# Who issues the weight loads of the late experts, when, and in which order, in a transformer block with routed experts

## The chip, the core and the metric

One Trainium2 chip, one core. The time is that of one execution on the device, in microseconds (us); lower is better. The engines are named as in the profile: PE (TensorE), DVE (VectorE), ACT (ScalarE), POOL (GpSimd) and SP (SyncE). DMA transfers are moved by 16 DMA engines that all queues share; q1 is the queue that SP issues into, q10 that of ACT, q0 that of POOL.

## The reference, cut to what matters

```python
x = x + attention(x) @ Wout.T                     # 16 sequences of 256 tokens, D = 256, 16 heads of 64
tok = x.reshape(-1, d)                            # 4096 tokens
gate = softmax(tok @ Wgate.T)                     # E = 8 experts
vals, idx = top_k(gate.T, bs // E)                # every expert takes its 512 best tokens
g = layernorm(tok[idx]) * mlp_g + mlp_b
y = gelu(einsum('ked,ehd->keh', g, fc1s) + b1s)   # 256 -> 1024
y = einsum('keh,edh->ked', y, fc2s) + b2s         # 1024 -> 256
tok = tok.at[idx].add(y * vals)
```

All numbers are float32. fc1 and fc2 of one expert are 1 MB each, b2 is spread over the partitions to 128 KB.

## The kernel before

The first 760 us are attention, ordered by a plan with a long table of places; at its end the routing finds each expert's tokens in two halves, so that there are 16 **jobs**: jobs 0 to 7 are the eight experts on their first 256 tokens, jobs 8 to 15 the same experts on the second 256. Job 0 is in the plan too; jobs 1 to 15 are a loop written out by hand (L1569 to L1622).

A job has 16 **slots**. In slots 0 to 7 `up` (L1273, tile `ph`) multiplies by fc1, 4 matmul passes each, and ACT follows with `gelu` (L1285, tile `hid`). In slots 8 to 15 `down` (L1293, tile `py`) multiplies by fc2, first for the job's tokens 0 to 127, then for the others; DVE finishes each half (L1304, `y`) and POOL adds it to `out` in DRAM with an indirect DMA (`scatter`, L1310). While job k computes, the tokens of job k+1 are brought:

- `list_matmul` (L1186, `pls`) and `take` (L1195) make the list of tokens. For the late jobs, k+1 from 9 to 15 (the flag `exchanged`), this is in slot 0; for the earlier ones in slot 5 (slot 7 once).
- `gather` (L1202, `xg`): two indirect DMAs by POOL, 128 tokens each.
- The tokens must be turned. Early jobs do it on PE in slot 14 (`transposes`, L1211, `px`). Late jobs do it by an **exchange** in slot 6: DVE turns blocks of 32 (`turn`, L1236, `xb`), SP writes them to DRAM (`away`, L1243, `xblocks`) and reads them back across the partitions in pieces of 512 bytes (`back`, L1250, `xT`). In slot 13 ACT scales `xT` (`affine`, L1258), in two halves; the next job's first `up` needs the first of them.

`load` (from L1138) brings a job's weights: fc2 into `w2`, which takes one of two buffers of the attention's tag `oT`; fc1 into `w1`, one of two buffers of tag `v`; then b2. It stands at the end of job k for job k+2 (`far`), when the buffers of job k have just come free, and all of it is issued by SP. SP works in order: a DMA that waits for its buffer holds all that stand behind it. The loads of jobs 0 and 1 are in the plan, that of job 2 ahead of the loop.

Of the kernel before, what the change touches and what calls it, by code (L numbers as in the profile page):

```python
# [9 lines left out]
F32 = mybir.dt.float32  # L10
# [8 lines left out]
P = 128  # L19
B, N, D = 16, 256, 256  # L20
# [9 lines left out]
FC = DD // P  # L30
# [16 lines left out]
class Plan:  # L47
# [7 lines left out]
    def step(self, place, engine, took, run, needs=(), makes=(), tiles=(), mode=0, lag=0.1):  # L55
        k = len(self.steps)
        self.steps.append((place, engine, took, run, needs, tiles, mode, lag))
        for m in makes:
            self.makers.setdefault(m, []).append(k)
# [7 lines left out]
def kernel(  # L67
# [18 lines left out]
    nc = tc.nc  # L86
# [338 lines left out]
    if True:  # L425
# [4 lines left out]
        moe = ctx.enter_context(tc.tile_pool(name="moe", bufs=2))  # L430
# [79 lines left out]
        class Through:  # L510


            def load(self):
                self.w = {}
                for c in range(DC):
                    self.w[c] = work.tile([P, H * HD], F32, tag="prT", bufs=4, name="wn")
                    nc.sync.dma_start(self.w[c], woutN[bass.ts(c, P), :])
# [614 lines left out]
        class Job:  # L1132
# [2 lines left out]
                self.oh = self.xT = None  # L1135
                self.exchanged = False

            def load(self):  # L1138


                e = self.e
                self.w2 = seq.tile([P, FC, D], F32, tag="oT", name="w2")
                nc.sync.dma_start(self.w2, fc2T[e].rearrange("(f p) d -> p f d", p=P))
                self.w1 = seq.tile([P, DC, DD], F32, tag="v", bufs=2, name="w1")
                rows = fc1Q if self.exchanged else fc1T
                nc.sync.dma_start(self.w1, rows[e].rearrange("(c p) f -> p c f", p=P))
                self.b2 = moe.tile([P, D], F32, tag="b2", bufs=2, name="b2")
                nc.sync.dma_start(self.b2, b2s[:, bass.ts(e, D)].to_broadcast([P, D]))

            def gives(self, engine=nc.vector):  # L1150

# [201 lines left out]
        for b in range(B):  # L1353
# [20 lines left out]
            else:  # L1374
                mr, xT_, wide, rows, hT = ("mr", b), ("xT", b), ("wide", b), ("rows", b), ("hT", b)
                f = base + FIRST[0]
# [36 lines left out]
            for d in range(HP // 2):  # L1413
                a = Quad(b, d)
                p = base + d * QUAD
# [25 lines left out]
            for t in range(TB):  # L1441
                a = Tail(b, t)
                p = base + TAIL[t]
# [60 lines left out]
        for n in range(2):  # L1504
            a = jobs[n]
            k = top + 10 + 20 * n
# [4 lines left out]
            for i in range(10):  # L1511
                name, took, by = {"D": ("DVE", 0.49, nc.vector), "P": ("POOL", 2.55, nc.gpsimd), "A": ("ACT", 2.1, nc.scalar)}[who[i]]
# [9 lines left out]
            for c in range(DC):  # L1522
                name, took, by = ("ACT", 0.55, nc.scalar) if c == 0 or n else ("DVE", 0.48, nc.vector)
# [4 lines left out]
        k = top + 30  # L1528
# [26 lines left out]
        def lay_out(job):  # L1555

            job.gives()
            for a in list(range(0, 18, 2)) + list(range(18, NT, 3)):
                yield
                job.onehot(a, a + (2 if a < 18 else 3))  # L1560
# [8 lines left out]
        for k in range(1, len(jobs)):  # L1569
            a = jobs[k]  # L1570
            new = jobs[k + 1] if k + 1 < len(jobs) else None
            far = jobs[k + 2] if k + 2 < len(jobs) else None
            late = k == last + 1
            list_at = LATE_AT if late else LIST_AT if new and new.exchanged else 5
            for s in range(SLOTS):
                for step in next(rest, ()):
                    step()
                if late and s == 0:
                    new.gives()
                if late and s < 6:  # L1580
                    new.onehot(6 * s, 6 * s + 6)
                if new and s == list_at:
                    for _ in () if late else parts:
                        pass
                    new.list_matmul(0, NT)
                    new.take()
                    new.gather()
                    if k == 1:
                        jobs[0].scatter(by_end[1])
                if s == 0:  # L1590
                    for step in held:
                        step()
                    held = []
                if new and new.exchanged:
                    for what in EXCHANGE.get(s, ()):
                        getattr(new, what)()
                elif new and s == TURN_AT:
                    new.transposes()
                    new.evict()
                if not late and s < list_at:  # L1600
                    next(parts, None)
                if far and k != last and s > list_at:
                    if s == list_at + 1:
                        parts = lay_out(far)
                    for _ in range(2 if far.exchanged and list_at else 1):
                        next(parts, None)
                if s < FC:
                    a.up(s)
                    a.gelu(s)
                    if s == FC - 1:  # L1610
                        a.weigh()
                else:
                    i, q = divmod(s - FC, 4)
                    a.down(i, 2 * q, 2 * q + 2)
                    if q == 3:
                        a.finish(i)
                        if far and far.exchanged and i == KL - 1:
                            held = [partial(a.scatter, i)]
                        else:
                            a.scatter(i)  # L1620
            if far:
                far.load()  # L1622
        assert next(rest, None) is None

# [57 lines left out]
```

## Time and profile before

| | |
|---|---|
| median of 3 runs | 1033.66 us (1032.98 to 1035.72) |
| profiled execution | 1033.8 us, of which the trace spans 1032.1 |
| PE busy | 998.3 us (97%) |
| DVE, POOL, ACT busy | 812.1, 657.4, 569.6 us |
| the loop of jobs (first `up` of job 0 to the last `down`) | 774 to 1022 us |
| jobs 9 to 15 and job 8 ahead of them | 900 to 1022 us |

The rest of the span, from 1022 us on, is the last scatters and the end of the program. The time of the profiled execution lies 0.14 us above the median, and 1.7 us of it lie outside the traced span.

### The profile page before, as it was taken

To read this page: it belongs to the slowest core of one execution; us is meant where nothing else is said; L and a number is where in the kernel's file an instruction comes from. 1 tells how busy PE (TensorE), PEld (TensorE's weight loads), DVE (VectorE), ACT (ScalarE), POOL (GpSimd) and SP (SyncE) were. 2 spreads that over 40 slices of the span, in tenths; PEclk is the share of its full clock that TensorE was granted. 3 is DMA by queue.
4 is the path that set the end of the run, shared out by engine and by line. 5 is a ranking of instruction groups with operands and counts; after the bars stand their busy time and mean duration, and the time that the engine had idled before them with its cause. 6 is when DMAs were issued, how large, how long until landed. Compare 5 with 4: busy or idle time off the path is not lost. (4 is left out here: it accounts for less than half of the span.)

```text
span 1032.1 us, 21313 instructions
## 1 busy us (share of the span) xinstructions
PE 998.3 (97%) x6803; PEld 606.7 (59%) x6803; DVE 812.1 (79%) x2271; ACT 569.6 (55%) x1596; POOL 657.4 (64%) x1003
## 2 busy tenths in 40 slices
PE   8999999999999999999999999998689999999996
PEld 6434455454554545455454545565468888888885
DVE  3789998899988889888898999887875888654630
ACT  2577766767667675766756766775214223233231
POOL 3699788788878787887878787765223333333332
PEclk9999999999999999999999999999889999999998
DMA  8456676676766767676776777677033557468662
GB/s 288 111 138 169 167 186 163 176 176 169 187 167 164 169 174 186 167 176 164 182 189 163 186 179 171 152 195 221 11 108 121 149 180 207 139 221 244 196 199 30
DMA packets 166144, 174.02 MB, mean 169 GB/s; under 512 B 18832, under 2 KB 154768, under 8 KB 166032
## 3 DMA queue, kind: packets, MB, share of 16 engines
q1 hardware_dynamic: 158512, 162.88, 58.8%
q0 software_dynamic: 6144, 8.39, 4.4%
q10 hardware_dynamic: 1376, 1.38, 0.4%
q8 instruction: 55, 0.90, 0.4%
q14 instruction: 57, 0.47, 0.1%
HBM read 59.57 MB, written 14.45 MB: 72 GB/s over the span
## 5 line engine op out<-in xcount | busy, mean ns | idle before, releaser
L441 PE MATMUL pm<-wq,hT 128*64 128x512 f32 x1536 | 352.7, 596 | 3.2 <-DVE qk L706 2.3
L787 ACT ACTIVATE pr<-sc,nmax 128x256 f32<-128x256 f32 x512 | 237.7, 479 | 119.7 <-DVE nmax L774 77.7
L798 POOL TENSOR_SCALAR pr<-pr,sums 128x256 f32<-128x256 f32 x512 | 237.5, 483 | 66.7 <-DVE sums L794 49.1
L112 POOL TENSOR_TENSOR ss<-ss,neghalf 128x8 f32<-128x8 f32 x128 | 210.8, 1647 | 10.7
L441 PEld LDWEIGHTS pm<-wq,hT 128*64 128x64 f32 x1536 | 106.5, 137 | 184.2 <-issue 146.3
L774 DVE TENSOR_REDUCE nmax<-sc 128x2 f32<-128x512 f32 x256 | 166.6, 670 | 11.3 <-PE sc L766 10.9
L808 DVE STREAM_TRANSPOSE pb<-pr 128x512 f32<-128x512 f32 x248 | 167.9, 692 | 6.5 <-POOL pr L798 5.8
L766 PE MATMUL sc<-kT,qT 64*128 64x256 f32 x1024 | 133.0, 392 | 0.6 <-ACT pr L787 0.6
L848 PE MATMUL po<-prT,v 128*64 128x256 f32 x1024 | 130.4, 384 | 0.1
L441 PE MATMUL pw<-wo,oT 128*64 128x264 f32 x1024 | 127.3, 391 | 0.5 <-DVE qk L706 0.5
L766 PEld LDWEIGHTS sc<-kT,qT 64*128 64x128 f32 x1024 | 93.8, 186 | 57.9 <-issue 24.8
L1310 POOL DMA_INDIRECT out<-y,idx x32 | 51.2, 1599 | 119.1 <-DVE oh L1178 55.8
L1273 PE MATMUL ph<-xT,w 128*128 128x256 f32 x512 | 118.8, 388 | 1.9 <-ACT xT L1258 1.9
L689 ACT ACTIVATE sq<-pm 128x512 f32<-128x512 f32 x128 | 77.2, 604 | 75.7 <-PE pm L441 74.9
L1293 PE MATMUL py<-w,hid 128*128 128x256 f32 x512 | 115.2, 380 | 0.4 <-ACT hid L1285 0.4
L848 PEld LDWEIGHTS po<-prT,v 128*64 128x64 f32 x1024 | 72.6, 137 | 68.8 <-issue 37.9
L693 DVE TENSOR_REDUCE ss<-sq 128x8 f32<-128x512 f32 x128 | 85.6, 670 | 32.8 <-ACT sq L689 32.0
L787 ACT ACTIVATION_READ_ACCUMULATOR pr<-sc,nmax 128x1 f32 x512 | 107.4, 210 | 0.0
L1273 PEld LDWEIGHTS ph<-xT,w 128*128 128x128 f32 x512 | 96.0, 192 | 16.1 <-ACT xT L1258 2.8
L1293 PEld LDWEIGHTS py<-w,hid 128*128 128x128 f32 x512 | 96.1, 190 | 13.6 <-ACT hid L1285 0.5
L706 DVE TENSOR_TENSOR qk<-pm,ss 128x512 f32<-128x512 f32 x128 | 86.9, 679 | 20.8 <-POOL ss L112 19.3
L1285 ACT ACTIVATE hid<-ph,vec 128x256 f32<-128x256 f32 x128 | 60.3, 474 | 74.2 <-PE ph L1273 65.1
(152 smaller groups left out, 1008.1 us busy)
## 6 DMA issues: line engine op xcount, KB each, us to landing
prT<-pb SPq DMA_DIRECT2D x496, 128.0 KB
qraw<-kb SPq DMA_DIRECT2D x128, 128.0 KB
kT<-kb SPq DMA_DIRECT2D x128, 128.0 KB
w<-in_fc2T SPq DMA_DIRECT2D x16, 1024.0 KB
w<-in_fc1T SPq DMA_DIRECT2D x9, 1024.0 KB
w<-in_fc1Q SPq DMA_DIRECT2D x7, 1024.0 KB
xT<-in_xT SPq DMA_DIRECT2D x16, 256.0 KB
out<-tok SPq DMA_DIRECT2D x32, 128.0 KB
```

What stands on the lines that cost most here:

```text
L112: nc.gpsimd.tensor_tensor(dst, src, neghalf[:, : src.shape[1]], ALU.pow)
L441: nc.tensor.matmul(out[cols], weights[:, cols], moving, start=start, stop=stop)
L693: nc.vector.tensor_reduce(self.ss[:, 0, :], self.sq.rearrange("p (q e d) -> p e q d", q=QB, e=8), AX.XY, ALU.add,)
L706: nc.vector.tensor_tensor(self.qk.rearrange("p (q e d) -> p q e d", q=QB, e=8), self.pm.rearrange("p (q e d) -> p q e d", q=QB, e=8), by_h ...
L766: nc.tensor.matmul(self.sc[i, j][:, t, :], qTs[self.b][rows, hp, bass.ts(t, P)], keys[rows], start=True, stop=True,)
L774: nc.vector.tensor_reduce(self.nmax[i, j], self.sc[i, j], AX.X, ALU.max, negate=True)
L787: nc.scalar.activation(dst, src, AF.Exp, bias=self.nmax[i, j][:, t : t + 1], scale=1.0, accum_out=self.sums[i][:, 0, j, t : t + 1],)
L798: nc.gpsimd.tensor_scalar(self.pr[i, j][:, t, :], self.pr[i, j][:, t, :], self.sums[i][:, 1, j, t : t + 1], 1.0, ALU.mult, ALU.mult,)
L808: nc.vector.transpose(self.pb[i][:, :, :, j].rearrange("p k c t n -> p t k c n"), self.pr[i, j].rearrange("p t (k c m) -> p t k c m", c=TB ...
L848: nc.tensor.matmul(self.po[j * HD : (j + 1) * HD, i, :], vs[self.b][:, c, bass.ts(4 * self.d + 2 * i + j, HD)], prT[:, j, c] if (self.b, s ...
L1273: nc.tensor.matmul(self.ph[f], self.w1[:, c, bass.ts(f, P)], self.xT[:, :, c].rearrange("p k i n -> p k (i n)") if self.exchanged else sel ...
L1293: nc.tensor.matmul(self.py[i], self.hid[:, f, bass.ts(i, P)], self.w2[:, f, :], start=(f == 0), stop=(f == FC - 1),)
```

## The change

`load` takes the queue as an argument and issues fc1, then fc2, then b2. For jobs 9 to 15 it is called in the ninth slot (s == 8) of the job ahead, on ACT's queue, in place of the end of the job before that one, on SP's. The calls for jobs 0 to 8 stay where they are and on SP; for them the order of fc1 and fc2 alone changes.

```diff
-            def load(self):
+            def load(self, queue=nc.sync):
                 e = self.e
                 self.w2 = seq.tile([P, FC, D], F32, tag="oT", name="w2")
-                nc.sync.dma_start(self.w2, fc2T[e].rearrange("(f p) d -> p f d", p=P))
                 self.w1 = seq.tile([P, DC, DD], F32, tag="v", bufs=2, name="w1")
+                self.b2 = moe.tile([P, D], F32, tag="b2", bufs=2, name="b2")
                 rows = fc1Q if self.exchanged else fc1T
-                nc.sync.dma_start(self.w1, rows[e].rearrange("(c p) f -> p c f", p=P))
-                self.b2 = moe.tile([P, D], F32, tag="b2", bufs=2, name="b2")
-                nc.sync.dma_start(self.b2, b2s[:, bass.ts(e, D)].to_broadcast([P, D]))
+                queue.dma_start(self.w1, rows[e].rearrange("(c p) f -> p c f", p=P))
+                queue.dma_start(self.w2, fc2T[e].rearrange("(f p) d -> p f d", p=P))
+                queue.dma_start(self.b2, b2s[:, bass.ts(e, D)].to_broadcast([P, D]))
...
                 else:
+                    if s == FC and new and new.exchanged and k > 1:
+                        new.load(nc.scalar)
                     i, q = divmod(s - FC, 4)
                     a.down(i, 2 * q, 2 * q + 2)
...
-            if far:
+            if far and not far.exchanged:
                 far.load()
```

On ACT, from the gelus of job 7 on, before (`hid` is written by the eight gelus of a job, `xT` by the two halves of `affine`):

```order
L1285 ACTIVATE hid<-ph,vec 128x256 x8
L1258 ACTIVATE xT<-xT,vec 128x4x64 x2
L1285 ACTIVATE hid<-ph,vec 128x4x2x32 x8
L1258 ACTIVATE xT<-xT,vec 128x4x64 x2
L1285 ACTIVATE hid<-ph,vec 128x4x2x32 x8
```

and now, from the gelus of job 8 on:

```order
L1285 ACTIVATE hid<-ph,vec 128x256 x8
L1146 DMA w_11209<-in_fc1Q 128x2x1024
L1147 DMA w_11208<-in_fc2T 128x8x256
L1148 DMA b_11210<-in_b2s 128x256
L1258 ACTIVATE xT<-xT,vec 128x4x64 x2
L1285 ACTIVATE hid<-ph,vec 128x4x2x32 x8
```

Three DMA issues now stand between a job's last gelu and the `affine` of the next job's tokens, in seven jobs.

On SP, the end of its program before; the first three rows load job 8, the next three job 9, and so on in turns with the exchange:

```order
L1143 DMA w_10923<-in_fc2T 128x8x256
L1146 DMA w_10925<-in_fc1T 128x2x1024
L1148 DMA b_10927<-in_b2s 128x256
L1143 DMA w_11107<-in_fc2T 128x8x256
L1146 DMA w_11109<-in_fc1Q 128x2x1024
L1148 DMA b_11111<-in_b2s 128x256
L1243 DMA xblocks<-xb 128x512
L1250 DMA xT<-xblocks 128x4x128
L1143 DMA w_11257<-in_fc2T 128x8x256
L1146 DMA w_11259<-in_fc1Q 128x2x1024
L1148 DMA b_11261<-in_b2s 128x256
```

and now:

```order
L1146 DMA w_10924<-in_fc1T 128x2x1024
L1147 DMA w_10923<-in_fc2T 128x8x256
L1148 DMA b_10925<-in_b2s 128x256
L1243 DMA xblocks<-xb 128x512
L1250 DMA xT<-xblocks 128x4x128
L1243 DMA xblocks<-xb 128x512
L1250 DMA xT<-xblocks 128x4x128
```

After job 8's weights SP issues nothing but the fourteen DMAs of the exchanges.

On SP at the end of attention, the load of job 1 between the last stores of the block's tokens (`tn`, `tok`), before:

```order
L904 DMA xn_dram<-tn 128x256 x2
L1143 DMA w_9204<-in_fc2T 128x8x256
L1146 DMA w_9206<-in_fc1T 128x2x1024
L1148 DMA b_9208<-in_b2s 128x256
L894 DMA out<-tok 128x256 x2
```

and now:

```order
L904 DMA xn_dram<-tn 128x256 x2
L1146 DMA w_9205<-in_fc1T 128x2x1024
L1147 DMA w_9204<-in_fc2T 128x8x256
L1148 DMA b_9206<-in_b2s 128x256
L894 DMA out<-tok 128x256 x2
```

fc1, which needs a buffer of `v`, no longer stands behind fc2, which needs one of `oT`; the same swap is made in the loads of jobs 2 to 8.

## Rows read from the trace of the kernel before

**Rows 1.** The page: busy time of the engines, their share of the span.

```profile
PE 998.3 (97%) x6803; PEld 606.7 (59%) x6803; DVE 812.1 (79%) x2271; ACT 569.6 (55%) x1596; POOL 657.4 (64%) x1003
```

**Rows 2.** Timeline of PE, jobs 8 to 15: start, us, what [idle before, releaser].

```profile
900.83 7.15 PE L1273 MATMUL ph<-xT,w 128*128 128x256 f32 x32
...
914.73 0.95 PE L1186 MATMUL pls<-give,oh 128*128 128x10 bf16 x32
915.54 7.15 PE L1273 MATMUL ph<-xT,w 128*128 128x256 f32 x32
...
931.46 7.23 PE L1273 MATMUL ph<-xT,w 128*128 128x256 f32 x32 [1.08 <-ACT xT L1258]
...
977.45 8.92 PE L1273 MATMUL ph<-xT,w 128*128 128x256 f32 x32 [0.34 <-ACT xT L1258]
...
993.92 7.15 PE L1273 MATMUL ph<-xT,w 128*128 128x256 f32 x32
...
1008.42 7.23 PE L1273 MATMUL ph<-xT,w 128*128 128x256 f32 x32 [0.44 <-ACT xT L1258]
```

**Rows 3.** The chain that ended last: start, us, what.

```profile
902.74 6.34 DMA xg<-xn_dram,idx
...
924.53 3.25 DMA xblocks<-xb
...
930.81 0.61 ACT xT L1258
```

**Rows 4.** Stretches: busy us by engine, granted PE clock, DMA share, GB/s.

```profile
909.00:915.00 6.00, 6.00 (x39) 5.21 (x38) 5.42 (x29) 0.61 (x2) 1.56 (x1) 1.00 0.31 93
...
979.00:981.00 2.00, 2.00 (x6) 1.55 (x6) 0.32 (x2) 0.74 (x2) 0.92 (x1) 0.50 1.03 365
```

**Rows 5.** Timeline of SP's queue during job 8.

```profile
900.22 0.37 SPq L1143 DMA_DIRECT2D w<-in_fc2T  x1
...
909.57 0.34 SPq L1243 DMA_DIRECT2D xblocks<-xb  x1
911.67 0.38 SPq L1250 DMA_DIRECT2D xT<-xblocks  x1
```

**Rows 6.** Timeline of POOL during job 8: the two gathers.

```profile
901.44 0.99 POOL L1202 DMA_INDIRECT xg<-xn_dram,idx  x1 [2.71 <-DVE idx L1195]
902.74 0.95 POOL L1202 DMA_INDIRECT xg<-xn_dram,idx  x1 [0.30 <-issue]
```

**Rows 7.** The tile xg from 760 us on: gathers whose landing is seen.

```profile
DMA to landing us min/median/max: 2.8/2.9/4.1
```

**Rows 8.** Timeline of ACT at the end of job 8.

```profile
914.39 1.09 ACT L1258 ACTIVATE xT<-xT,vec 128x256 f32<-128x256 f32 x2 [5.90 <-DMA xT<-xblocks]
```

**Rows 9.** Queues from 903 to 905.5 us: packets, MB, share of 16 engines.

```profile
q1 hardware_dynamic: 681, 0.94, 105.3%
```

**Rows 10.** Queues from 906 to 908 us, POOL's row.

```profile
q0 software_dynamic: 90, 0.25, 33.7%
```

**Rows 11.** Queues from 8.5 to 11 us, when SP and ACT both load weights.

```profile
q1 hardware_dynamic: 187, 0.68, 66.8%
q10 hardware_dynamic: 192, 0.35, 36.2%
```

**Rows 12.** Timeline of PE at job 0: last use of v, first of xg.

```profile
741.84 1.08 PE L848 MATMUL po<-prT,v 128*64 128x256 f32 x8
...
771.87 0.33 PE L1211 MATMUL px<-ident,xg 128*128 128x128 f32 x1 [0.26 <-DMA xg<-xn_dram,idx]
772.53 0.55 PE L1211 MATMUL px<-ident,xg 128*128 128x128 f32 x3 [0.33 <-DMA xg<-xn_dram,idx]
```

**Rows 13.** Timeline of SP's queue ahead of it: the load of job 1.

```profile
762.40 0.38 SPq L1143 DMA_DIRECT2D w<-in_fc2T  x1
```

**Rows 14.** Timeline of POOL: the second gather for job 5, in job 4.

```profile
845.46 0.97 POOL L1202 DMA_INDIRECT xg<-xn_dram,idx  x1 [0.30 <-issue]
```

**Rows 15.** Timeline of PE: the first use of what it brings.

```profile
850.24 0.60 PE L1211 MATMUL px<-ident,xg 128*128 128x128 f32 x4
```

## The prediction

> **What bounds the kernel now.** I read the page first: PE is busy 97% of the span [rows 1], so only time in which PE waits, or runs at its lower clock, can be won. The timeline of PE then shows where it does so in the jobs that the change touches. A job that nothing disturbs lasts 14.71 us (first `up` at 900.83, the next at 915.54) [rows 2]; the list matmuls between two jobs are 0.81 of it (914.73 to 915.54). Against that:
>
> - job 9 to 10: 915.54 to 931.46 is 15.92, 1.21 too long, 1.08 of it PE idle for ACT's `xT`;
> - job 10 to 13: 45.99 for three jobs of 14.71, 1.86 too long, again with a wait for `xT`;
> - job 13 to 14: 16.47, 1.76 too long. That job's `up` took 8.92 instead of 7.15: right after PE's waits the granted clock in it is 0.50 [rows 4], the 1.2 GHz level;
> - job 14 to 15: 14.50 where 13.90 was due (no list follows), 0.60 too long.
>
> Together 5.4 us, all begun by late tokens. The chain says why they are late: the gather of the next job's tokens took 6.34 us from the issue of its second half [rows 3], while gathers whose landing the trace can tell took 2.9 [rows 7]. SP had issued 2.1 MB of weights just ahead, from 900.22 [rows 5], the gathers came at 901.44 and 902.74 [rows 6]. From 903 to 905.5 the DMA engines were full and moved packets of SP's queue alone [rows 9]; POOL's came to move only from 906 on [rows 10]. From 909 to 915 the same engines were used 31% [rows 4]. The weights travel just when the gather needs the engines, and then the engines rest.
>
> **The late loads, moved.** I count from the first `up` of a job (900.83 = 0); the next job starts at 14.71.
>
> Today the gather's second half is issued at 1.91 [rows 6] and lands at 8.25, `away` goes out at 8.74, `back` at 10.84 [rows 5], ACT begins to scale at 13.56 [rows 8]. The first half of the scaling takes 0.61 [rows 3] and PE starts 0.04 later, so `xT` must have landed by 14.06. Job 8 met that by half a microsecond; the jobs above did not.
>
> With the weights gone from slot 0 the gather should land at 1.91 + 2.9 = 4.8, in a range from 4.7 (the 2.8 of rows 7) to 8.25 (no better than now). A DVE turn of about half a microsecond follows, as today (8.25 to 8.74), so `away` leaves at 5.3. It takes 2.1 (909.57 to 911.67) [rows 5], or 3.25 in the worst case [rows 3]; of the seven, two were above 3. `back` leaves at 7.4, or 8.55.
>
> ACT's last gelu of job 8 ended at 914.39 - 5.90 = 908.49, that is 7.66 [rows 8]. Then ACT issues fc1, fc2 and b2. ACT has nothing else before the scaling (it sat 5.90 us idle there), so the three issues, some 0.4 us each if they cost what SP's cost [rows 5], take nothing from the path. Without that cover they would delay what follows by 1.2 us per job. On SP the exchange no longer stands behind weights.
>
> So fc1 and `back` set out together, on two queues that share the engines. `back` alone takes 2.72 (911.67 to 914.39): landing at 10.1. What the weights add I bound from two sides. Nothing, if `back` goes ahead. At most about 3.4: that is what the weights added to the gather (6.34 - 2.9); and if the queues take turns packet by packet, `back` (32 pieces of 512 B for each engine) lets pass fc1 whole (16 pieces of 4 KB) and 16 of fc2's 1 KB pieces, 1.3 MB, at the 1.03 MB in 2.5 us of rows 11 some 3.2. At start-up, where SP and ACT load at once, the packets of the two queues moved 187 to 192 [rows 11], which is taking turns. `back` has a start of 0.3 us, so I take +2: landing at 12.1, at worst 13.5; both before 14.06. Only a slow `away` with the full 3.4 misses, by 14.65 - 14.06 = 0.6, in about two jobs of seven; with a chance of one more spell at the low clock I put 0.5 us aside.
>
> fc1 must be there at 14.71. `back` moves 0.26 MB in 2.72, of which 0.65 is data at the rate of rows 11, so a transfer costs some 2.1 beside its data; fc1 then lands at 7.7 + 2.1 + 2.6, plus 0.65 for `back`: 13.0. fc2 comes behind it, some 3.5 us later, and is first read at 14.71 + 7. Its tail ends about when the next gather is issued.
>
> Saved: 5.4 - 0.5 = 4.9.
>
> **The early loads, swapped.** On SP fc1 now waits for `v` alone. For job 1 that buffer is last read by the products at 741.84 [rows 12], while fc2's `oT` comes free at 762.40 [rows 13]. fc1 can go some 19 us sooner, and what meets the first gather shrinks by 1 MB, or 2.6 us of transfer. PE waited 0.26 and 0.33 us for that gather [rows 12]; DVE and ACT stood idle behind it. I count both: 0.6 (0 if the stores that follow the load hold the gather as long).
>
> In jobs 2 to 8 the same swap sends fc1 out at half of job k-2, when its last `up` ends, beside the gathers of slot 5. PE reads those in slot 14. The least room is in job 4: issue 845.46, read at 850.24, 4.78 us [rows 14, 15]. Alone the gather lands in 2.9 to 4.1; as slow as beside the weights it takes 6.34 and PE waits 1.6. The other jobs have more room. Bounds 0 and 1.6, taken 0.2, nearer to none, since fc1's large pieces let the gather in [rows 10].
>
> **Sum.** 4.9 + 0.6 - 0.2 = 5.3 us from the profiled execution's 1033.8, which gives 1028.5; the median of the runs shown is 0.14 lower: **1028.4**.
>
> **The rivals.**
>
> *Thin slack.* `back` pays the full 3.4 in every job, PE waits a few tenths in some, once or twice falls to the low clock (1.8 each), and job 5's gather costs its 1.6. Of the 6.0 won, 3 to 6 go back: 1030.6 to 1033.7. For it: the slack is half a microsecond in that case.
>
> *`back` stands behind all that ACT has queued* (the other side). The gathers were held while fc2 ran: no packet of theirs in 2.5 us [rows 9]. Today 8.9 us lie between the first issue and the landing of the gather behind it (900.22 to 909.08) [rows 3, 5]. If `back` is served last, it lands near 7.7 + 8.9 = 16.6, `up` starts at 17.25 and not 14.71: 2.5 us in each of seven jobs, 17.8. Then 1033.7 - 0.6 - 5.4 + 17.8 = 1045, and up to 1.8 per job more if each wait brings the clock down. It decides from a landing at 14.06, and makes the kernel slower from 14.06 + 0.9 on (six microseconds over seven jobs). Against it: fc1's pieces did let the gather pass [rows 10], and queues of SP and ACT shared evenly [rows 11].
>
> The Trainium skill ("DMA: Bandwidth & Descriptors", section "Queues, rings and completion order") says that an engine turns from queue to queue only after a whole packet, some 9 to 17 descriptors and at most 64. By it `back` waits for about one packet of fc1, 2.6 us, never for all: landing at 12.7, or 13.9 after a slow `away`, and this rival would fall out. The trace agrees for SP's and ACT's queues as far as 2.5 us can show [rows 11], but POOL's queue got no turn for as long [rows 9], so I leave the rival a chance.
>
> *fc1 comes too late.* It now leaves 7 us ahead of its use. If it took the 8.9 us that weights and gather take together, PE would wait 1.9 us in seven jobs, 13 us: 1041. Against it: the order, and the sum of 13.0.
>
> *No gain.* The gather is slow by itself, or its place is taken by the scatter and the tail of the loads: within 1 us of 1033.7. Against it: the 2.9 of rows 7.
>
> **How the numbers follow.** The forecast has 0.62 (its own range 1027.3 to 1030.3: all terms at their best give 6.0 + noise, or 3.4 of it), thin slack 0.17, `back` last 0.11, fc1 late 0.04, no gain 0.06. 0.3%, or 3.1 us, is about what a measurement of this kernel can tell from no change; faster than 1030.6 are the forecast and a quarter of thin slack: 0.66. Same: most of the rest of thin slack and the no gain, 0.19. Slower: 0.15. The range from 1027.0 to 1033.5 holds the forecast and thin slack and leaves out two in ten.
>
> **What would show it.** Right: gathers of jobs 9 to 15 land some 3 us after issue; `away` leaves near 5.3 of its job, not 8.7; ACT's scaling starts before 14.06; `up` of jobs 9 to 15 follow each other by 14.7 with no wait for `xT`; no stretch at 0.50 after 970 us; q10 carries about 15.5 MB more. Job 0's first `px` without a wait. Wrong: waits of PE for `xT` at every late job, with `back` taking 5 us or more; waits of `up` for fc1's DMA; waits of `px` for `xg` in jobs 1 to 6.

## The result and the profile after

The change made the kernel slower. Over seven runs of each, the median went from 1032.29 us (1029.03 to 1035.72) to 1040.87 us (1038.05 to 1046.11); the ratio is 1.0095, with a 95% interval of 1.0072 to 1.0119. The forecast was 1028.4, with 0.15 for slower. The profiled execution of the kernel after took 1038.67 us, of which the trace spans 1036.8, 4.7 more than before. It is one of four executions that took 1038.05 to 1040.87 at a mean granted clock of 0.988 to 0.990, while the other three took 1044.45 to 1046.11 at 0.980 to 0.982.

First the page of the kernel after: busy time by engine, which answers to [rows 1], and the queues (packets, MB, share of the 16 DMA engines).

```profile
PE 997.7 (96%) x6803; PEld 605.7 (58%) x6803; DVE 811.6 (78%) x2271; ACT 568.7 (55%) x1596; POOL 655.3 (63%) x1003
...
q1 hardware_dynamic: 148320, 147.28, 54.1%
q10 hardware_dynamic: 11568, 16.98, 4.8%
```

PE did the same work; the 4.7 us of this trace are all waiting. q10 carries 15.6 MB more, so the loads did move to ACT's queue. The timeline of PE in jobs 8 to 15 (compare [rows 2]) shows where PE waits:

```profile
900.89 7.15 PE L1273 MATMUL ph<-xT,w 128*128 128x256 f32 x32
...
918.23 7.23 PE L1273 MATMUL ph<-xT,w 128*128 128x256 f32 x32 [2.50 <-ACT xT L1258]
...
933.01 7.15 PE L1273 MATMUL ph<-xT,w 128*128 128x256 f32 x32
...
948.95 7.23 PE L1273 MATMUL ph<-xT,w 128*128 128x256 f32 x32 [1.10 <-ACT xT L1258]
...
963.73 7.15 PE L1273 MATMUL ph<-xT,w 128*128 128x256 f32 x32
...
980.72 8.92 PE L1273 MATMUL ph<-xT,w 128*128 128x256 f32 x32 [2.14 <-DMA xT<-xblocks]
...
997.19 7.15 PE L1273 MATMUL ph<-xT,w 128*128 128x256 f32 x32
...
1013.23 7.23 PE L1273 MATMUL ph<-xT,w 128*128 128x256 f32 x32 [1.98 <-ACT xT L1258]
```

Four of the seven late jobs, every second one, wait one to two and a half microseconds for `xT`; after the third wait `up` ran partly at the low clock (8.92). From the first `up` of job 8 to that of job 15 it is 112.34 us (900.89 to 1013.23), against 107.59 before (900.83 to 1008.42) [rows 2]: 4.75 more, the whole difference of the spans. The chain that ended last shows which transfers took the time (start, us, what):

```profile
934.93 2.58 DMA xg<-xn_dram,idx
...
938.15 2.55 DMA xblocks<-xb
...
940.83 7.38 DMA xT<-xblocks
...
972.47 7.39 DMA xT<-xblocks
...
1005.03 7.47 DMA xT<-xblocks
```

The gather now takes 2.58 us, where it took 6.34 in the first late job before [rows 3]: that part of the forecast came true. But `back`, 2.72 us before, takes 7.4. The timeline of the queues (SPq, ACTq) and of ACT in job 10 shows the order of the issues:

```profile
940.26 0.37 ACTq L1146 DMA_DIRECT2D w<-in_fc1Q  x1
940.73 0.43 ACTq L1147 DMA_DIRECT2D w<-in_fc2T  x1
940.83 0.37 SPq L1250 DMA_DIRECT2D xT<-xblocks  x1
941.20 0.59 ACTq L1148 DMA_DIRECT2D b<-in_b2s  x1
...
948.30 1.09 ACT L1258 ACTIVATE xT<-xT,vec 128x256 f32<-128x256 f32 x2 [7.63 <-DMA xT<-xblocks]
```

fc1 went out 0.57 us ahead of `back`. And this is what the DMA engines moved (queue: packets, MB, share): first row from 941 to 944.5, the other two from 945 to 948.

```profile
q10 hardware_dynamic: 242, 0.99, 80.6%
...
q10 hardware_dynamic: 758, 0.78, 78.6%
q1 hardware_dynamic: 528, 0.26, 31.6%
```

For 3.5 us only ACT's queue moves, in pieces of 4 KB (242 packets, 0.99 MB): that is fc1. Not one of `back`'s 512 pieces is among them. fc2's 1 KB pieces follow, and from 945 on the two queues take turns; `back` ends after 2.5 us more, while fc2 still flows. So `back` is held, but not until the whole load is through. The same holds in all four slow jobs: the first piece of `back` moves 3.8 to 4.3 us after its issue, when 1.2 to 1.6 of the 2.1 MB have moved. In the three others it moves after 1.0 us, as it does in e8 below, where nothing is ahead:

| tokens of job | fc1 issued | `back` issued | `affine` starts | `back`'s issue to `affine` |
|---|---|---|---|---|
| 9 | 908.16 | 909.72 | 917.58 | 7.86 |
| 10 | 925.56 | 923.37 | 927.19 | 3.82 at most (ACT itself was still issuing) |
| 11 | 940.26 | 940.83 | 948.30 | 7.47 |
| 12 | 956.56 | 955.62 | 958.50 | 2.88 |
| 13 | 970.98 | 972.47 | 980.07 | 7.60 |
| 14 | 989.74 | 986.32 | 991.37 | 5.05 at most (as job 10) |
| 15 | 1004.44 | 1005.03 | 1012.58 | 7.55 |

Where fc1 is ahead, by 0.57 to 1.56 us, `back` takes 7.5 to 7.9; where `back` is ahead, it is through before. (For job 9 the profile names b2's landing as what ACT waited for; `affine` does not read b2, and in e4 below it starts 0.94 us after b2's issue, with 2 MB ahead of b2.) It alternates because the list and the gather stand in slot 0 in front of PE's wait, while the load hangs on slot 8 behind it: a job that starts 2 us late gives its gather those 2 us, and so `back` overtakes the load once. In job 8 the gather's second half is issued 1.90 us behind the first `up` (902.79), in job 9 0.71 us ahead of it (917.52).

### The profile page after: what moved, and what is told of

Read it like the earlier page. It is cut to its first block, busy times and chain, and to the rows that moved or that the text cites. A ratio compares the mean times of both kernels' runs of the same rounds, so it can differ in the third digit from the quotient of the medians.

```text
span 1036.8 us, 21329 instructions
## 1 busy us (share of the span) xinstructions
PE 997.7 (96%) x6803; PEld 605.7 (58%) x6803; DVE 811.6 (78%) x2271; ACT 568.7 (55%) x1596; POOL 655.3 (63%) x1003
## 4 chain that ended last, share of the span: by engine, by line
PE 65%; POOL 10%; DMA 8%; DVE 8%; issue 3%; ACT 2%; SPq 2%; POOLq 0%; ACTq 0%; DVEq 0%
PE pm L441 21%; PE sc L766 8%; PE ph L1273 8%; PE po L848 8%; PE pw L441 8%; PE py L1293 7%; POOL ss L112 4%; POOL pr L798 3%; DMA xT<-xblocks 2%; SPq L555 2%; DMA xg<-xn_dram,idx 2%; POOL hT L617 1%; DVE nmax L774 1%; DVE pb L808 1%; PE fill L454 1%
## 5 line engine op out<-in xcount | busy, mean ns | idle before, releaser
L1310 POOL DMA_INDIRECT out<-y,idx x32 | 51.1, 1598 | 121.9 <-DVE oh L1178 66.2
```

## The experiments

Three sums keep the tables short. *Early* is from the transposes (`px`) of job 1's tokens to the first `up` of job 8, *late* from there to the first `up` of job 15, each in the profiled execution, and *idle* is the time in which `up` waited in jobs 8 to 15. The attention ahead of them moves by up to 4 us from one execution to the next (the `px` of job 1 starts between 787.88 and 792.21 in these traces, at 789.02 in that of the kernel before), so that spans alone would mislead; the ratio is from all the runs.

| kernel | early | late | idle in `up`, on | median, us | ratio (95%) |
|---|---|---|---|---|---|
| before | 111.81 | 107.59 | 1.9 `xT` | 1032.29 beside after, 1033.41 beside e1 to e4, 1033.72 beside e5 to e8, 1034.17 beside e9 | 1 |
| after | 112.69 | 112.34 | 7.7 `xT` | 1040.87 | 1.0095 (1.0072 to 1.0119) |
| e1, order alone | 114.11 | 102.81 | 0.5 `xT` | 1030.73 | 0.9979 (0.9957 to 1.0001) |
| e2, place alone | 111.78 | 123.59 | 10.2 fc1, 2.6 `xT` | 1048.82 | 1.0149 (1.0111 to 1.0187) |
| e3, ninth slot on SP | 113.77 | 108.82 | 4.5 fc1 | 1034.75 | 1.0009 (0.9987 to 1.0030) |
| e4, ACT delayed | 113.61 | 110.48 | 4.9 fc1 | 1038.33 | 1.0061 (1.0035 to 1.0087) |
| e5, order, late jobs | 111.78 | 102.95 | 0.6 `xT` | 1029.98 | 0.9962 (0.9946 to 0.9978) |
| e6, behind `back` | 112.51 | 104.15 | 1.4 `xT` | 1033.01 | 0.9990 (0.9972 to 1.0009) |
| e7, fc1 alone on ACT | 113.24 | 105.73 | 1.8 `xT`, 1.0 fc1 | 1033.63 | 0.9995 (0.9977 to 1.0013) |
| e8, no late loads | 111.81 | 102.12 | 0.0 | 1029.78 | 0.9960 (0.9943 to 0.9976) |
| e9, half of fc1 on ACT | 113.45 | 103.84 | 1.3 fc1 | 1035.72 | 1.0012 (0.9990 to 1.0034) |

**e1: the order alone.** All loads stay on SP and at their old places; fc1 goes ahead of fc2.

```diff
                 self.w2 = seq.tile([P, FC, D], F32, tag="oT", name="w2")
-                nc.sync.dma_start(self.w2, fc2T[e].rearrange("(f p) d -> p f d", p=P))
                 self.w1 = seq.tile([P, DC, DD], F32, tag="v", bufs=2, name="w1")
+                self.b2 = moe.tile([P, D], F32, tag="b2", bufs=2, name="b2")
                 rows = fc1Q if self.exchanged else fc1T
                 nc.sync.dma_start(self.w1, rows[e].rearrange("(c p) f -> p c f", p=P))
-                self.b2 = moe.tile([P, D], F32, tag="b2", bufs=2, name="b2")
+                nc.sync.dma_start(self.w2, fc2T[e].rearrange("(f p) d -> p f d", p=P))
                 nc.sync.dma_start(self.b2, b2s[:, bass.ts(e, D)].to_broadcast([P, D]))
```

> One part alone: fc1 in front of fc2 and b2 in every load, all of them on SP at the places of before. Theory A (what hurts is that the exchange's read meets weights that ACT issued just ahead of it): the loss of the change is gone, since nothing stands on ACT's queue. fc1 then leaves in the middle of a job behind the exchange's read on the same queue, only fc2 and b2 are left beside the gather, so the gather takes 4 to 5 us and not 6.3, the read stays at 2.6 to 3.0: 3 to 5 us faster than before. Theory B (the swap is what hurts, since the large pieces of fc1 hold the engines): the read, which now has fc1 close behind it, takes over 5 us and the time is within 2 us of the changed kernel.

Measured: 1030.73, 2.7 us below before, with an interval that just reaches 1; theory A had 3 to 5. In the trace, 4.78 us are won late, nearly all that there is, and 2.3 are lost early. `back` takes 2.8 to 3.0 us, once 4.5, so theory B falls. The waits of `px` for the gather, from the timeline of PE:

```profile
771.98 0.55 PE L1211 MATMUL px<-ident,xg 128*128 128x128 f32 x3 [0.45 <-DMA xg<-xn_dram,idx]
...
820.05 0.86 PE L1211 MATMUL px<-ident,xg 128*128 128x128 f32 x4 [0.97 <-DMA xg<-xn_dram,idx]
...
899.66 0.55 PE L1211 MATMUL px<-ident,xg 128*128 128x128 f32 x3 [0.51 <-DMA xg<-xn_dram,idx]
```

Why it helps late: fc1's buffer comes free at half of a job, and on SP fc1 stands right behind `back` (issued at 911.58 and 912.04 in job 8, for job 10). Only fc2 is left for the end of the job, so that the gather meets 1 MB there and not 2: `away` leaves 4.5 to 7.0 us after the issue of the gather's second half, against 6.5 to 9.1 before. Why it hurts early: there fc1 now goes out among the gathers and scatters of POOL. The longest wait, the 0.97 us of job 2, came, by the order of the times, from a scatter (L1310). The timeline of POOL:

```profile
805.10 1.63 POOL L1310 DMA_INDIRECT out<-y,idx  x1 [4.92 <-DVE reach L999]
812.88 1.57 POOL L1310 DMA_INDIRECT out<-y,idx  x1 [6.15 <-issue]
...
816.07 0.97 POOL L1202 DMA_INDIRECT xg<-xn_dram,idx  x1 [0.30 <-issue]
```

From 805.1 to 810 no packet of POOL's queue moved, while fc2 (issued at 805.85) moved 0.79 MB. The next scatter left only at 812.88, and the gather behind it 10.4 us into the job, where before it was 7.1; from its issue to its use it then took 4.0.

**e2: the place alone.** The kernel after, with fc2 ahead of fc1.

```diff
-                queue.dma_start(self.w1, rows[e].rearrange("(c p) f -> p c f", p=P))
                 queue.dma_start(self.w2, fc2T[e].rearrange("(f p) d -> p f d", p=P))
+                queue.dma_start(self.w1, rows[e].rearrange("(c p) f -> p c f", p=P))
```

> The other part alone: late loads on ACT in the ninth slot, but fc2 first. Theory A: the read of the exchange is held by what lies ahead of it whatever the size of its pieces, 6 us or more where it is issued after the load; and fc1 comes last of 2 MB, some 8 us after its issue, so that PE also waits for fc1: as slow as the changed kernel or up to 10 us slower. Theory B (it is fc1's 4 KB pieces that hold the read): the read shares with fc2's 1 KB pieces from the start and takes 4 to 5 us; PE waits for fc1 alone, under 1 us a job.

Measured: 1048.82, the slowest of all, as theory A has it. Now PE waits for fc1, 10.2 us in all. In job 8 fc2 was issued at 911.26 and `back` 1.92 us later; the packets from 912 to 917:

```profile
q10 hardware_dynamic: 1158, 1.53, 91.7%
q1 hardware_dynamic: 9, 0.02, 0.9%
```

All of fc2 (1024 pieces of 1 KB) and half of fc1 pass. The 9 packets of SP's queue move before 913.2, when `back` has only just been issued; from then to 917 it moves none. ACT could scale at 920.82, 7.64 us after `back`'s issue. So small pieces ahead hold `back` as large ones do, and theory B falls.

**e3: the ninth slot on SP's queue.** The kernel after, the late loads issued by SP, where they stand behind `back`.

```diff
-                        new.load(nc.scalar)
+                        new.load(nc.sync)
```

> The changed kernel with the late loads in the same slot but issued by SP, so that they stand behind the exchange's read on one queue. Theory A: the read takes 2.6 to 3.0 us in every job, fc1 lands 4 to 5 us after its issue, no wait for xT is left: 4 to 6 us faster than before. Theory C (the engines simply have too much to move in that half of a job, whoever issues it): the read still takes 5 us or more, or PE waits for fc1 instead, and the time is near that of the changed kernel.

Measured: 1034.75, no difference from before that the runs can tell. `back` is quick again (911.65 to 914.45 in job 8), and no `up` waits for `xT`. But now fc1 is late. The timeline of PE:

```profile
918.75 7.15 PE L1273 MATMUL ph<-xT,w 128*128 128x256 f32 x32 [1.30 <-issue]
...
949.88 7.14 PE L1273 MATMUL ph<-xT,w 128*128 128x256 f32 x32 [1.59 <-DMA w<-in_fc1Q]
...
995.85 8.83 PE L1273 MATMUL ph<-xT,w 128*128 128x256 f32 x32 [1.62 <-DMA w<-in_fc1Q]
```

fc1 was issued at 912.08 and `up` started at 918.75, 6.67 us later (the profile names no releaser for this wait; `xT` had been scaled by then). That is A for the read and C for fc1: from behind `back`, fc1 does not reach PE in time in three of the seven jobs. The time is nearer to that of before than either theory had it.

**e4: ACT's issue delayed.** The kernel after, with nine small copies on ACT ahead of each late load, so that the load goes out behind `back` on a queue of its own.

```diff
+        idle = route.tile([P, 16], F32, name="idle")
...
                     if s == FC and new and new.exchanged and k > 1:
+                        for _ in range(9):
+                            nc.scalar.copy(idle, vec[:, :16])
                         new.load(nc.scalar)
```

> The changed kernel with nine small copies on ACT ahead of each late load (they write a tile that nothing reads), so that ACT issues the load some 2 us later, behind the read of the exchange. Theory A, by which the one that is issued first is served first: the read takes about 3 us in every job, waits for xT vanish, fc1 lands 1 us or less ahead of its use: 3 to 6 us faster than before. Theory D (ACT's queue is served ahead of SP's whenever both have work): the read still takes 5 us or more, and the time is that of the changed kernel or up to 5 us more.

Measured: 1038.33. The timeline of job 8:

```profile
910.86 0.38 SPq L1250 DMA_DIRECT2D xT<-xblocks  x1
911.69 0.38 ACTq L1146 DMA_DIRECT2D w<-in_fc1Q  x1
...
913.70 1.09 ACT L1258 ACTIVATE xT<-xT,vec 128x256 f32<-128x256 f32 x2 [1.88 <-DMA xT<-xblocks]
```

0.83 us of lead are enough: `back` takes 2.84. Leads of 0.53 and 0.34 in later jobs are enough too (2.94 and 2.67). So neither the second queue nor ACT as issuer slows it, but what was issued ahead: A holds for the read, and D falls. The 3 to 6 us of gain that A promised did not come: what is won on the read is lost on fc1, as in e3. It came to use at 918.60, 6.91 after its issue, with PE waiting 1.57.

**e5: fc1 first, in the late jobs only.** The kernel before, with e1's order for job 1 and jobs 10 to 15; `load_w1`, `load_w2` and `load_b2` are the three parts of `load`, for fc1, fc2 and b2.

```diff
-            def load(self):
...
+            def load(self, fc1_first=False):
+                if fc1_first:
+                    self.load_w1()
+                    self.load_w2()
+                else:
+                    self.load_w2()
+                    self.load_w1()
+                self.load_b2()
...
-            at(ROUTE + 60 + n * 80, "SP", 1.9, jobs[n].load, (), [(1, "w", n)], [("oT", B + n), ("v", B + n)], lag=-1.0)
+            at(ROUTE + 60 + n * 80, "SP", 1.9, partial(jobs[n].load, n == 1), (), [(1, "w", n)], [("oT", B + n), ("v", B + n)], lag=-1.0)
...
-                far.load()
+                far.load(k + 2 > 9)
```

> The kernel before, all loads on SP and at their old places; fc1 is issued ahead of fc2 for job 1 and jobs 10 to 15 alone. Theory (the order of the two weights is where a gain lies, and only late in the program): jobs 8 to 15 follow each other as with the swap everywhere, 102.8 us from the first up of job 8 to that of job 15 and not 107.6; the waits for gathers that the swap brought to jobs 2 to 8 (up to 0.97 us) are gone, so job 8 starts at about 900.3. Ratio to before about 0.995, near 1028.5 us. Rival (the swap wins nothing late that it doesn't lose elsewhere, the 4.8 us were one good execution): 0.998 or above.

Measured: 1029.98, ratio 0.9962, as the theory has it; it is faster than both kernels. Early is as before (111.78), late 102.95. The timeline of PE holds one wait:

```profile
973.18 7.15 PE L1284 MATMUL ph<-xT,w 128*128 128x256 f32 x32
988.64 7.23 PE L1284 MATMUL ph<-xT,w 128*128 128x256 f32 x32 [0.61 <-ACT xT L1269]
```

**e6: everything behind `back`.** SP issues, in the ninth slot of job k, fc2 and b2 of job k+1 and fc1 of job k+2; `load` is split in three as in e5.

```diff
...
+                    if s == FC and new and new.exchanged:
+                        new.load_w2()
+                        new.load_b2()
+                        if far:
+                            far.load_w1()
...
-            if far:
+            if far and not far.exchanged:
                 far.load()
+            elif k == last + 1:
+                far.load_w1()
```

> Loads of the late jobs issued by SP in the ninth slot, behind back: there fc2 and b2 of the next job, then fc1 of the job after it, so that nothing large moves while a gather or back does, and fc1 has a whole job of time. Theory (the aim of the change was sound, what failed is that back was issued behind the load and that fc1 had too little time): gathers land about 3 us after issue, back takes 2.7 to 3.0, no up waits for xT or fc1, 14.7 us per job, 103 us from job 8 to 15, ratio about 0.995. Rival (loads beside back or in front of the next gather cost something wherever they stand): waits of up for xT remain, ratio 1.00.

Measured: 1033.01, between the theory and the rival: late, 3.4 us are won, but waits for `xT` stay, and the ratio doesn't tell the kernel from before. The stretches 917 to 921 and 921 to 924 of the trace (busy time by engine, granted clock, DMA share, GB/s) show why:

```profile
917.00:921.00 4.00, 4.00 (x20) 3.54 (x19) 1.75 (x10) 1.89 (x4) 1.99 (x2) 1.00 0.91 318
921.00:924.00 3.00, 3.00 (x16) 2.64 (x15) 0.54 (x2) 1.76 (x4) 0.61 (x1) 1.00 0.27 92
```

The 2.1 MB set out at 911.28 and fill the engines until about 921, while the next job's gather, issued at 918.39, waits: `away` leaves at 924.26, 5.87 us after that issue. From `back` (issued at 910.87) to that gather it is 7.5 us, and the weights take nearly ten: here both do not fit between the two.

**e7: fc1 alone on ACT.** The kernel after, with fc2 and b2 on SP's queue behind `back`.

```diff
                 queue.dma_start(self.w1, rows[e].rearrange("(c p) f -> p c f", p=P))
-                queue.dma_start(self.w2, fc2T[e].rearrange("(f p) d -> p f d", p=P))
-                queue.dma_start(self.b2, b2s[:, bass.ts(e, D)].to_broadcast([P, D]))
+                nc.sync.dma_start(self.w2, fc2T[e].rearrange("(f p) d -> p f d", p=P))
+                nc.sync.dma_start(self.b2, b2s[:, bass.ts(e, D)].to_broadcast([P, D]))
```

> The kernel after, with fc1 alone on ACT's queue in the ninth slot; fc2 and b2 go on SP behind back. Theory A (back gets no packet until the transfer that was queued ahead of it has moved, then shares with what follows): where fc1 is ahead, back starts when fc1's packets end, as before about 3 to 3.5 us late, but then has the engines alone or is ahead of fc2 on its own queue, so it takes 5.5 to 6 us and not 7.4 to 7.8; waits of up for xT shrink from 2.1 to 2.6 to some 0.5 to 1; ratio about 1.003. Theory B (back shares evenly with fc2 and fc1 and is slow because 2 MB are queued): with half of them it takes 4 to 4.5 us, no wait, ratio below 1. Theory C (the number of queues or ACT as issuer holds it, not the bytes): 7.4 as in the kernel after.

Measured: 1033.63, no difference from before. The timeline of job 13:

```profile
985.25 0.37 ACTq L1146 DMA_DIRECT2D w<-in_fc1Q  x1
985.80 0.38 SPq L1250 DMA_DIRECT2D xT<-xblocks  x1
...
992.99 1.09 ACT L1258 ACTIVATE xT<-xT,vec 128x256 f32<-128x256 f32 x2 [7.32 <-DMA xT<-xblocks]
```

And the packets from 985.8 to 989 (first row), and from 989 to 990.5:

```profile
q10 hardware_dynamic: 189, 0.77, 81.1%
...
q1 hardware_dynamic: 483, 0.26, 56.0%
q10 hardware_dynamic: 80, 0.27, 44.8%
```

Again nothing of `back` until fc1 has nearly all moved. Over the five jobs in which fc1 led, by 0.03 to 1.87 us, `back` took between 4.65 and 7.46 us; counted from fc1's issue, `affine` began after 6.5 to 7.7 us each time. In the two jobs in which `back` led, by 0.37 and 0.53, it took 3.3 and 3.1. That is theory A, with its size off: 5.5 to 6 was expected, three of five jobs took more and two less. Two of them come near C's 7.4, but the packets show the hold ending with fc1, and in e4 ACT's queue holds nothing. In the job with a lead of only 0.03 us the queues did take turns (199 packets of q1 and 204 of q10 from 927 to 929.5), and `back` was no sooner there: 7.46 us. Turns piece for piece, 512 B against 4 KB, cost as much as waiting.

**e8: no late loads.** Jobs 9 to 15 compute with job 8's fc1, fc2 and b2, so their part of the output is another one.

```diff
-            if far:
+            if far and not far.exchanged:
                 far.load()
+            elif far:
+                far.w1, far.w2, far.b2 = jobs[8].w1, jobs[8].w2, jobs[8].b2
```

> The kernel before, with no loads for jobs 9 to 15: they compute with job 8's fc1, fc2 and b2, so their outputs are not the reference's. It bounds what any place and order of these loads can win. Theory: gathers take 3 us, back 2.7, no wait in jobs 9 to 15, 14.7 us per job, ratio about 0.995, 5 us of gain at most. Rival (gathers or back are slow by the scatters beside them, or by themselves): waits for xT stay, less than 2 us of gain.

Measured: 1029.78, ratio 0.9960. The groups of PE by line, 899 to 1023 us (busy, mean ns, idle before):

```profile
L1273 PE MATMUL ph<-xT,w 128*128 128x256 f32 x256 | 57.1, 382 | 0.0
```

No `up` waits, and late is 102.12: 5.47 us below before. By these traces that is all that any place of these loads can win, and e5 has 4.64 of it; by the runs it is 3.9 us, and e5 has 3.7. `away` still takes up to 4.1 us here (908.13 to 912.22), so its slow cases are not the loads' doing.

**e9: half of fc1 ahead.** As e7, but ACT issues only the first half of fc1, 0.5 MB; the rest goes on SP behind `back`.

```diff
-                queue.dma_start(self.w1, rows[e].rearrange("(c p) f -> p c f", p=P))
-                queue.dma_start(self.w2, fc2T[e].rearrange("(f p) d -> p f d", p=P))
-                queue.dma_start(self.b2, b2s[:, bass.ts(e, D)].to_broadcast([P, D]))
+                halves = rows[e].rearrange("(c p) f -> p c f", p=P)
+                queue.dma_start(self.w1[:, 0], halves[:, 0])
+                nc.sync.dma_start(self.w1[:, 1], halves[:, 1])
+                nc.sync.dma_start(self.w2, fc2T[e].rearrange("(f p) d -> p f d", p=P))
+                nc.sync.dma_start(self.b2, b2s[:, bass.ts(e, D)].to_broadcast([P, D]))
```

> The kernel after, with only the first half of fc1 (0.5 MB) issued by ACT in the ninth slot; the second half, fc2 and b2 go on SP behind back (in the early jobs fc1 travels as two halves too, both on SP). Theory (back gets no packet until what was issued ahead of it on the other queue has moved, so its delay follows the bytes ahead): where ACT is ahead, back lands about 1.3 us earlier after the load's issue than with the whole fc1 ahead, at 5.2 to 5.6 us after it and not 6.5 to 7.7, some 13 us after the job's first up, so waits of up for xT nearly vanish; what is left are waits for fc1's second half, which has 6 to 7 us from behind back to its use: up to 1 us in the jobs where back is late. From job 8 to 15 104 to 106 us. Rival (back is held a fixed 3 us whenever anything is ahead): it takes 6.5 to 7.5 us again, waits for xT stay at 0.5 to 1 us, 106 us or more.

Measured: from the half's issue to `affine` 4.8 to 6.7 us, 5.6 in the mean (5.46, 5.83, 5.83, 5.90, 6.73, 4.79, 4.88), against 6.5 to 7.7 with the whole fc1 ahead and 8.0 to 9.4 with fc1, fc2 and b2 ahead in the kernel after. From 0.5 to 1 MB ahead the delay grows, by 1.4 us in the mean, and the rival's fixed 3 us fall: the first piece of `back` moves 1.5 to 2.4 us after its issue here, 2.4 to 3.9 in the held jobs of e7. Beyond 1 MB the hold grows little more: it is 3.8 to 4.3 in the kernel after and 3.9 in e2, and ends while the load still flows. No `up` waits for `xT`; the waits that are left are for fc1's second half:

```profile
950.55 6.71 PE L1275 MATMUL ph<-xT,w 128*128 128x256 f32 x30 [0.55 <-DMA w<-in_fc1Q]
...
980.90 6.71 PE L1275 MATMUL ph<-xT,w 128*128 128x256 f32 x30 [0.70 <-DMA w<-in_fc1Q]
```

The median isn't below before all the same. Early, the order takes 1.6 of the 3.75 us back; the profiled execution (1034.28) lies below the median of its kind, 1035.72, and what the others lost beyond it is not in a trace.

## Why the prediction was wrong

**The step that failed** is the price of `back` beside fc1. The text took +2 us, with +3.4 as the upper bound, so that `xT` would land 12.1 us after the job's first `up`, at worst 13.5, before the deadline of 14.06. In job 8 ACT could scale only 16.69 us after it (917.58 - 900.89), in the other slow jobs 15.3 to 16.3. The issues and the wait of job 8:

```profile
906.01 0.34 SPq L1243 DMA_DIRECT2D xblocks<-xb  x1
908.16 0.38 ACTq L1146 DMA_DIRECT2D w<-in_fc1Q  x1
...
909.72 0.38 SPq L1250 DMA_DIRECT2D xT<-xblocks  x1
...
917.58 1.09 ACT L1258 ACTIVATE xT<-xT,vec 128x256 f32<-128x256 f32 x2 [9.02 <-DMA b<-in_b2s]
```

Two terms of that sum were off. `back` took 7.4 to 7.9 us where 4.7, at most 6.1, had been taken. And the start of 0.3 us that the sum gave `back` did not exist: in the slow jobs fc1 left 7.25 to 7.27 us after the first `up`, not 7.7, since ACT issued it while its last gelu was still running (908.08 to 908.55 in job 8). `away` took 2.7 to 3.7 us, not 2.1, so that `back` left after 7.8 to 8.8 us and not 7.4, behind fc1. In e4 and e7 leads of 0.34 us and more were enough, and with one of 0.10 in e2 `back` took 3.75 at most (964.37 to 968.12); by these runs a start like the one in the sum would have served. Why `away` took longer is not shown; without late loads (e8) it took 2.1 to 4.1.

The rival "`back` stands behind all that ACT has queued" had put the landing at 16.6, from the 8.9 us that gather and weights took together [rows 3, 5]; the same span, load issued to `xT` there, measured 9.42, 8.04, 9.09 and 8.14 us in the four slow jobs. The rival had the right place, and its price, an `up` at 17.25, is near the 17.34 of job 8 and 0.3 to 1.3 above the other three. It was not right in all: `back` did not wait for the whole load, and only every second job meets the load ahead, where the rival had all seven. It was given 0.11.

The step rested on two readings. One was the packets of q1 and q10 at start-up, 187 to 192, read as a rule for the two queues [rows 11]. But those two were both in full flow; how a queue fares that starts while the other is flowing was in other rows, those of the gather, which got no packet in 2.5 us [rows 9]. They were read as a weakness of POOL's queue. e2, e7 and e9 show it for SP's queue too; e4 and the jobs of e7 in which `back` led show that the order of issue decides, but for the one job of e7 with a lead of 0.03 us. The other reading was the upper bound itself: +3.4 was thought of as all that can happen, while in job 10 `back` lost 4.7 (7.4 against 2.72). Its first piece moved 4.3 us after the issue, where a read that stands alone needs 1.0, which is 3.2 of the loss; its pieces then took 2.5 us in turns with fc2, where those of e8's first read took 1.2.

The Trainium skill ("DMA: Bandwidth & Descriptors", section "Queues, rings and completion order") has an engine turn to the next queue after a packet of some 9 to 17 descriptors, at most 64; by the prediction's estimate from that, `back` was to wait 2.6 us and land at 12.7. The held jobs of e7, where the hold ended with fc1, would fit it, but e2 doesn't: in e2 the queue went on from fc2's pieces of 1 KB to fc1's of 4 KB (0.5 of the 1.53 MB from 912 to 917) with `back` issued at 913.18 and still without a turn, though one packet must have ended between the two by that rule; ACT could scale at 16.8 of that job (920.82 - 903.99).

**fc1's own time** was a third term off. It was put at 5.35 us from issue to landing (2.1 + 2.6 + 0.65). In the kernel after it doesn't show, since fc1 there goes ahead of `back`. Where it goes behind, in e3 and e4, it took 6.67 and 6.91 in the first job and 5.1 to 7.8 over all jobs in which `up` waited for it. In none of e3, e4 and e7 were both needs met in every job, `back` first and fc1 within 7 us of its use. e3 and e4 lose 1.2 and 2.9 us late by it; e7 wins 1.9 late and gives 1.4 back early. e9, with half of fc1 ahead, comes nearest (3.75 won late).

**The clock.** One wait of 2.14 us was followed by an `up` of 8.92 us, 1.76 over the rule; from 980 to 984 the granted clock was 0.66 in the mean:

```profile
980.00:984.00 4.00, 3.28 (x9) 2.55 (x10) 1.97 (x11) 1.56 (x3) 2.67 (x3) 0.66 0.35 76
```

The rival had foreseen up to one such spell a job; in the profiled execution there was one, as there was one before.

**What held.** The gather lands as summed: `away` leaves 5.1 us after the first `up` (906.01 - 900.89), 5.3 was forecast. The loss in the late jobs was put at 5.4 us; with no loads 5.47 come back (e8). ACT's three issues delayed nothing in front of a needed scaling. The order of job 1's load gave 0.5 of the 0.6 (first `pls` to the second `px` of job 0: 762.26 to 772.53 before, 761.95 to 771.71 after).

**The early order** was taken at 0.2 us, bounds 0 to 1.6. It costs 0.9 in the kernel after, 1.4 to 2.3 in e1, e3, e4, e7 and e9, and nothing in e2 and e5, which keep the old order there (111.78 both). e6 keeps it too, but its fc1 of job 9 goes out at 893.07, and the gather there makes PE wait 0.51. The wait came in job 2, not in job 4, where the least room was seen: the gather issued at 813.76 meets fc1 of job 4, issued at 813.55. fc1's large pieces did not let it in, as the prediction had it: from 815 to 817.5 SP's queue moved 185 packets and POOL's none.

**The sum, mended**, against the profiled execution before: late +4.75 in place of -4.9, early -0.5 +0.9 in place of -0.4, makes 1033.8 + 5.2 = 1039.0; 1038.67 was measured. These terms are read from the same two traces, so the sum shows only that little else changed between them. The medians are 8.6 us apart; what the other executions lost beyond the 4.9 of this pair is in no trace, and where they lost it stays open. And the change's two halves were judged the wrong way round: the order, put at nothing in the late jobs, is worth 4.8 us there (e1); the place, put at 4.9 won, turns that into the loss of 4.75.

## What to carry to other kernels

When a small transfer on the path and a large one that can wait are issued at the same time, let the small one be issued first, by order on one queue or by some tenths of a microsecond of lead; a second queue doesn't protect it. That is shown for a read that SP issues: a scatter that POOL began to issue 0.75 us ahead of fc2 was held all the same (e1). Price a transfer that starts behind others by a row in which just that happens, on whatever queue, and not by rows in which both queues are already flowing. And try the parts of a change one by one: here a swap of two lines was the gain, and it came in the late jobs, where the gather is not issued in the same place.

## What the runs showed of the hardware

- A read of 256 KB in 512 B pieces, issued 0.03 to 1.9 us behind a load on another queue, was through 4.8 to 6.7 us after that load's issue with 0.5 MB ahead (e9), 6.5 to 7.7 with 1 MB (e7), 8.0 to 9.6 with 2.1 MB (the kernel after and e2); issued 0.34 us or more ahead, it took 2.7 to 3.3, about as without a load.
- With 2.1 MB ahead its first piece moved 3.8 to 4.3 us after its issue, against 1.0 alone, whether the load led by 0.57 or by 1.92 us, and with 1.2 to 1.7 MB of the load moved by then.
- It is not settled what holds it: the traces show that no packet of it moves, not where it stands. Nor is the one job of e7 explained in which a lead of 0.03 us gave turns from the start.
- A 1 MB load with a 256 KB read in front of it reached the matmul that waited for it 5.1 to 7.8 us after its issue (e3, e4), though 1 MB alone is some 2.5 us of data at the 0.21 MB per 0.5 us that fc1 moves in full flow.
